# Two attention blocks: the seventh product of the output projection by quarter products

## The chip, the core and the metric

The kernel runs on one core of one Trainium2 chip. Its engines work side by side and wait for one another by semaphores: TensorE (PE in the profile, with its weight loads as PEld), VectorE (DVE), ScalarE (ACT), GpSimd (POOL) and the queue that issues transfers (SPq). Matrix products land in PSUM[...]; operands and results lie in SBUF. The metric is the time of the whole program on the device, in microseconds, median of several runs. Before the change it is 3261.11 us (three runs, 3260.39 to 3261.24).

## What is computed

Two layers of the same kind run one after the other on eight images of 512 channels and 32 x 32 points (N = 1024 tokens), all in float32:

```python
def layer(x, gn_scale, gn_bias, qkv_w, qkv_b, proj_w, proj_b):   # cut to one layer
    xn = group_norm(x) * gn_scale + gn_bias                      # 8 groups, or 32 in the second layer
    q, k, v = split(einsum('oc,bcn->bon', qkv_w, xn) + qkv_b)    # 8 heads of 64
    attn = softmax(einsum('bhdi,bhdj->bhij', q, k) / 8)
    out = einsum('bhij,bhdj->bhdi', attn, v)
    return einsum('oc,bcn->bon', proj_w, out) + proj_b + x       # the output projection
```

The change touches the last line only: the output projection, a product of a 512 x 512 matrix and a 512 x 1024 matrix.

## The kernel before

The kernel goes through 16 units, one for each layer and image. A unit makes q, k and v of its image, then the output projection of the unit before, then its own attention. So there are 15 such projections; that of the last unit is made by another routine with plain products.

Each of q, k, v and the projection is a product of matrices cut into 2 x 2 blocks, made with seven block products instead of eight (the scheme of Strassen and Winograd). A block product is, as it stands, four matmuls of 128 x 128 by 512 columns:

```python
    def block_product(bank, a, b, tokens, start, stop, between=None):
        for i in range(4 if tokens else 2):
            if i == 1 and between is not None:
                between()
            if tokens:
                dst = bank[:, i // 2, (i % 2) * FD2 : (i % 2 + 1) * FD2]
            else:
                dst = bank[:, i, :]
            for c in range(2):
                at, moving = (b, a) if tokens else (a, b)

                nc.tensor.matmul(
                    dst, at[:, c, ts(i, P)], moving[:, c, :],
                    start=start and c == 0 and not (tokens and i % 2),
                    stop=stop and c == 1, skip_group_check=True,
                )
```

Some of the seven are cut into 2 x 2 once more and made by seven quarter products, each one matmul of 256 columns. `INNER` says which:

```python
    INNER = {"q": (2, 5, 4, 3), "k": (1, 2, 7, 5, 4, 3), "o": (2, 3, 4)}
```

The quarter products of one block product go through `inner_products`:

```python
        def inner_products(bank, k, first=False):

            if k not in inner:
                products(bank, k, first, k != 5)
                return None
            a, b, one, two, order, room = inner[k]
            one, two, rest = one[:, 0, :FD2], two[:, 0, :FD2], room(f"m{k}_{name}")
            dst = {
                1: one, 6: one, 7: one, 5: two,
                2: bank[:, 0, :FD2], 3: bank[:, 0, FD2:], 4: bank[:, 1, :FD2],
            }
            to = {
                1: rest[:, 0, :FD2], 6: rest[:, 0, FD2:], 7: rest[:, 1, :FD2], 5: rest[:, 1, FD2:]
            }

            def step(j):
                nc.tensor.matmul(
                    dst[j], a[j], b[j], start=j in (1, 5) or first and j in (2, 4),
                    stop=j not in (1, 6), skip_group_check=True,
                )
                if j in to:
                    taken.append(nc.scalar.copy(to[j], dst[j]))

            for j in order if k != 1 else order[:-1]:
                step(j)
            return (rest, partial(step, order[-1])) if k == 1 else rest

        def fold(rest):
            add = nc.gpsimd.tensor_add
            add(rest[:, 0, FD2:], rest[:, 0, FD2:], rest[:, 1, FD2:])
            add(rest[:, 1, FD2:], rest[:, 1, :FD2], rest[:, 1, FD2:])
```

Quarters 2, 3 and 4 add straight into the bank of the block product. Quarters 1, 6 and 7 go one after the other into the same 256 columns of another bank (`one`), and 5 into a third (`two`). After each of those four ScalarE copies ("takes") what stands there into a room in SBUF, because the partial sums are wanted one by one: 1, 1+6, 1+6+7 and 5. `fold` has GpSimd add the four parts up, and `rests` has it add them to the result. The orders in use are

```python
    ORDER, ORDER_5, ORDER_1 = (1, 2, 3, 6, 5, 4, 7), (1, 5, 2, 6, 3, 4, 7), (2, 3, 1, 4, 5, 6, 7)
```

The first product of k, which uses `ORDER_1`, holds its last quarter back until two matmuls of the next product have gone (`order[:-1]` and `between`). The seven block products follow in this order (those branches that the projection doesn't take are cut):

```python
        bx, by, bz = apair[0], sbank[0], apair[1]
        ...
            products(bx, 1, True, False, between)
            ...
            p1 = work(accpool, "acc", "p1")
            nc.scalar.copy(p1, bx)
            done(sums)
            products(by, 6, True, False)
        u2 = work(*u2_in, "u2")
        summed(0, u2, by, p1)
        done(sums)
        rest = inner_products(bx, 2, fresh)
        c11(bx, p1 if fresh else None, rest)
        add_rest(0, 0, rest)
        done(sums)
        seventh = inner_products(by, 7)
        u3 = work(*u3_in, "u3")
        summed(1, u3, by, p1)
        if seventh is not None:
            fold(seventh)
        done(sums)
        twice = inner_products(bz, 5, True)
        others(1, 1, bz, u3, twice)
        add_rest(1, 1, twice, u3)
        if seventh is not None:
            rests(1, 1, seventh)
        done(sums)
        rest = inner_products(by, 4)
        others(1, 0, by, p1)
        add_rest(1, 0, rest)
        if seventh is not None:
            rests(1, 0, seventh)
        done(sums)
        rest = inner_products(bz, 3)
        others(0, 1, bz, u2, twice)
        add_rest(0, 1, rest, u2 if twice is not None else None)
        if twice is not None:
            rests(0, 1, twice)
        done(sums)
        return taken[-1:]
```

In the projection itself, `c11` and `others` add on VectorE a bank to what is there already; `plus` adds residual and bias; `rests` adds the parts on GpSimd and stores:

```python
        def done(sums):

            nonlocal g
            g += 1
            for i in range(2):
                if g == 2:
                    u2 = sums[1][:, i, :]
                    plus(u2, i, w.res[i][:, FD:], u2)
                elif g == 4:
                    u3 = sums[2][:, i, :]
                    plus(u3, 2 + i, w.res[2 + i][:, FD:], u3)
                elif g == 5:
                    p1 = sums[0][:, i, :]
                    plus(p1, 2 + i, w.res[2 + i][:, :FD], p1)
            after(g)

        results = {}

        def store(o, h):
            nc.sync.dma_start(dst[o * P : (o + 1) * P, ts(h, FD)], results[o, h])

        def c11(bank, *_):
            for i in range(2):
                cols = results[i, 0] = w.res[i][:, :FD]
                plus(cols, i, bank[:, i, :], cols)

        def others(r, h, bank, more, _=None):
            for i in range(2):
                o = 2 * r + i
                results[o, h] = more[:, i, :]
                w.evac[h] = nc.vector.tensor_add(more[:, i, :], bank[:, i, :], more[:, i, :])
                if (r, h) == (1, 1):
                    store(o, h)

        def rests(r, h, rest, _):
            for i in range(2):
                o = 2 * r + i
                cols = results[o, h]
                nc.gpsimd.tensor_add(cols, cols, rest[:, i, :])
                store(o, h)

        w.evac = [None, None]
        x, z, s1 = apair[0], apair[1], sbank[1]
        tmp = room_of(tmppool, "tmp")
        plan = {
            2: (s1, z, ORDER, tmp), 4: (x, s1, ORDER, tmp), 3: (s1, x, ORDER, room_of(accpool, "acc"))
        }
        inner = {k: (*w.inner_o[k], *plan[k]) for k in w.inner_o}
        w.taken = blocks(
            f"o_{w.u}", w.left, w.right_o, False, c11, others, done, (rbpool, "rb"), plain_sum, inner, rests
        )
```

The right factors of the quarters are differences that VectorE makes while v is being projected (numbers such as 20 and 21 in `parts` count the block products done so far: q has 1 to 7, then k 8 to 14, v 15 to 21). The left factors (`lefts`, three per block product) come from memory, where they were put once per layer:

```python
        parts = {
            3: [lambda: reciprocals(CC - 1)], 10: [lambda: divide(CC - 1)], 14: [bias_last],
            17: mixing[:2], 21: [mixing[3], mixing[2]],
        }

        w.inner_o = {}
        l, _ = units[u]
        src = inner_left[l]["o"].rearrange("p k s o -> p (k s) o")
        lefts = []

        def load_left():
            n = 2 * FD // P
            t = trpool.tile([P, n, P], F32, tag="tr", name=f"lo_{u}")
            lefts.extend(t[:, i, :] for i in range(n))
            if u == B:

                w.making = mix_inner_left(l, {"o": left_o})
            else:
                nc.sync.dma_start(t, src[:, :n, :])

        def make_left(i):
            w.making[i](lefts[3 * i : 3 * i + 3], later=behind_loads)

        def mix_o(k):
            tag = {2: "x2", 3: "x1", 4: "x4"}[k]
            room = tpool.tile([P, 4, FD2], F32, tag=tag, name=f"ro{k}_{u}")
            if k == INNER["o"][-1]:
                w.inner_o[k] = mix_inner_in(w.right_o[k], room, nc.vector)
                lefts.append(room[:, 3, :P])
                if u == B:
                    make_left(2)
                else:
                    nc.sync.dma_start(lefts[-1], src[:, len(lefts) - 1, :])
            else:
                w.inner_o[k], subs = mix_inner(w.right_o[k], room, nc.vector)
                for part in subs:
                    part()

        def finish():
            for i, k in enumerate(INNER["o"]):
                w.inner_o[k] = (inner_lefts(k, w.left[k], lefts[3 * i : 3 * i + 3]), w.inner_o[k])

        parts[15] = [load_left]
        if u == B:
            parts[20] = [partial(make_left, 0), partial(make_left, 1)]
        parts[18] = [partial(mix_o, 2)]
        parts[21] += [partial(mix_o, 4), partial(mix_o, 3)]
        w.finish = finish
        return parts
```

Of the kernel before, what the change touches and what calls it, by code (L numbers as in the profile page):

```python
# [11 lines left out]
F32 = mybir.dt.float32  # L12
# [20 lines left out]
def fast_path(ctx, tc, x, qkv_wT, proj_wT, vecs, groups, out, flag):  # L33
# [26 lines left out]

    INNER = {"q": (2, 5, 4, 3), "k": (1, 2, 7, 5, 4, 3), "o": (2, 3, 4)}
    assert D == H and C == FD
# [635 lines left out]
    def project(w, after):  # L698
# [29 lines left out]
        def store(o, h):  # L728
            nc.sync.dma_start(dst[o * P : (o + 1) * P, ts(h, FD)], results[o, h])
# [6 lines left out]
        def others(r, h, bank, more, _=None):  # L736
            for i in range(2):
                o = 2 * r + i
                results[o, h] = more[:, i, :]
                w.evac[h] = nc.vector.tensor_add(more[:, i, :], bank[:, i, :], more[:, i, :])  # L740
                if (r, h) == (1, 1):
                    store(o, h)

        def rests(r, h, rest, _):
            for i in range(2):
                o = 2 * r + i
                cols = results[o, h]
                nc.gpsimd.tensor_add(cols, cols, rest[:, i, :])
                store(o, h)

# [3 lines left out]
        plan = {  # L754
            2: (s1, z, ORDER, tmp), 4: (x, s1, ORDER, tmp), 3: (s1, x, ORDER, room_of(accpool, "acc"))
        }
# [31 lines left out]
    def attention(w, at_step, at_end):  # L788
# [188 lines left out]
        def bias_last():  # L977
# [6 lines left out]
            3: [lambda: reciprocals(CC - 1)], 10: [lambda: divide(CC - 1)], 14: [bias_last],  # L984
            17: mixing[:2], 21: [mixing[3], mixing[2]],
        }
# [19 lines left out]
        def mix_o(k):  # L1006
            tag = {2: "x2", 3: "x1", 4: "x4"}[k]
            room = tpool.tile([P, 4, FD2], F32, tag=tag, name=f"ro{k}_{u}")
            if k == INNER["o"][-1]:
                w.inner_o[k] = mix_inner_in(w.right_o[k], room, nc.vector)  # L1010
                lefts.append(room[:, 3, :P])
                if u == B:
                    make_left(2)
                else:
                    nc.sync.dma_start(lefts[-1], src[:, len(lefts) - 1, :])
            else:
# [7 lines left out]

        parts[15] = [load_left]
        if u == B:
            parts[20] = [partial(make_left, 0), partial(make_left, 1)]
        parts[18] = [partial(mix_o, 2)]
        parts[21] += [partial(mix_o, 4), partial(mix_o, 3)]
        w.finish = finish  # L1030
# [453 lines left out]
```

## Time and profile before

| | |
|---|---|
| time, median of 3 runs | 3261.11 us |
| span of the profiled run | 3260.1 us |
| granted TensorE clock | 1.00 |
| matmuls of quarter products, mean of one record | 379 ns (256 columns) |
| matmuls of whole block products of the projection | 592 ns (512 columns) |
| copies of quarter parts by ScalarE, projection | 180, 372 ns each |
| additions of parts by GpSimd, projection: folds of 256 columns | 90, 735 to 756 ns each on the mean |
| the same: additions of 512 columns to the result | 90, 1268 to 1673 ns each on the mean |

How to read the lines shown later: a line of the timeline gives the start in us from the beginning of the span, the length in us, the engine, the line of the kernel, the operation, what is written and read, and in brackets how long the engine stood idle before and what released it. Neighbouring instructions of one kind are merged, with their number after an x. One float32 matmul of the program leaves two records. Matmuls overlap in the pipeline, so the length of one record is more than the distance to the next. `s` and `a` are banks of PSUM, `m_o` the room for the parts of the projection, `u_o` and `p_o` its sums, `ro` and `lo` right and left factors of quarters. A wait line gives who waited for whom, the total in us, how many times, and the longest.

### The profile page before, as it was taken

Reading aid. Unit: us, or ns where it says so; the run is one execution under the profiler, and the core shown is the slowest. Engines: PE = TensorE matmul, PEld = TensorE weight load, DVE = VectorE, ACT = ScalarE, POOL = GpSimd, SP = SyncE. Lnnn points to the kernel's source line nnn. Section 1 sums busy time; section 2 is a strip of 40 time slices with the busy share of each in tenths; the row PEclk is TensorE's granted clock in tenths of the full one; section 3 lists DMA queues with packets and bytes.
Section 4 is the critical chain, followed back from the end, with each engine's and each line's share of the span. In section 5 each row is a group of like instructions: output and inputs, shape, how many; then the busy total and the mean of one; then the engine's idle time right before and its main releaser. Section 6 shows DMA issues by size and latency. Waiting matters only on the chain.

```text
span 3260.1 us, 56861 instructions
## 1 busy us (share of the span) xinstructions
PE 3247.2 (100%) x22206; PEld 1858.1 (57%) x22206; DVE 2713.7 (83%) x3460; ACT 1650.7 (51%) x2296; POOL 1238.9 (38%) x1235
## 2 busy tenths in 40 slices
PE   9999999999999999999999999999999999999999
PEld 5456474654746547465474655747556474564743
DVE  5887978889788897889978889797897978979777
ACT  1653726536274463744637446374563735637354
POOL 2054071531706317065470632607226071350710
PEclk9999999999999999999999999999999999999999
DMA  3112120121201212023120121201212012120221
GB/s 102 43 52 79 44 78 28 49 79 46 79 28 45 79 46 87 20 71 107 58 89 29 45 80 52 85 15 45 86 46 85 15 49 82 46 85 15 70 74 48
DMA packets 86465, 192.53 MB, mean 59 GB/s; under 512 B 22960, under 2 KB 34992, under 8 KB 84272
## 3 DMA queue, kind: packets, MB, share of 16 engines
q1 hardware_dynamic: 86192, 188.82, 17.0%
q8 instruction: 180, 2.95, 0.4%
q14 instruction: 93, 0.76, 0.1%
HBM read 148.00 MB, written 39.19 MB: 57 GB/s over the span
## 4 chain that ended last, share of the span: by engine, by line
PE 97%; DVE 1%; issue 1%; ACT 0%; DMA 0%; SPq 0%; DVEq 0%; ACTq 0%
PE a L851 26%; PE s L823 25%; PE s L419 14%; PE a L419 12%; PE a L458 10%; PE s L458 9%; PE a L823 1%; DVE acc L870 1%; PE s L769 0%; PE a L769 0%; PE s L364 0%; DVE tr L883 0%; DMA xn<-x_dram 0%; DVE acc L868 0%; ACT p L831 0%
## 5 line engine op out<-in xcount | busy, mean ns | idle before, releaser
L831 ACT ACTIVATE p<-s 128x1024 f32<-128x1024 f32 x976 | 997.0, 1023 | 560.4 <-PE s L823 526.3
L851 PE MATMUL a<-p,v 64*64 64x512 f32 x8192 | 1098.2, 589 | 1.7 <-ACT p L831 1.5
L823 PE MATMUL s<-q,k 64*64 64x512 f32 x7808 | 1056.4, 590 | 0.0
L870 DVE TENSOR_TENSOR acc<-acc,p 128x1024 f32<-128x1024 f32 x768 | 964.0, 1255 | 71.1 <-ACT p L831 18.1
L851 PEld LDWEIGHTS a<-p,v 64*64 64x64 f32 x8192 | 381.0, 131 | 500.5 <-ACT p L831 352.8
L823 PEld LDWEIGHTS s<-q,k 64*64 64x64 f32 x7808 | 380.1, 133 | 435.3 <-issue 425.6
L1080 POOL TENSOR_TENSOR r<-xn 128x256 f32<-128x256 f32 x30 | 51.2, 1707 | 1126.3 <-DVE acc L870 1049.0
L653 POOL TENSOR_TENSOR k<-k,m_k 128x512 f32<-128x512 f32 x180 | 259.7, 1464 | 0.0
L868 DVE TENSOR_TENSOR acc<-p,p 128x1024 f32<-128x1024 f32 x128 | 157.6, 1231 | 23.0 <-ACT p L831 13.9
L883 DVE STREAM_TRANSPOSE tr<-acc 128x1024 f32<-128x1024 f32 x128 | 157.9, 1233 | 0.0
L315 POOL TENSOR_TENSOR y<-var,half 128x4 f32<-128x4 f32 (+1 forms) x17 | 33.1, 1949 | 327.2 <-DVE var L313 327.2
L653 POOL TENSOR_TENSOR q<-q,m_q 128x512 f32<-128x512 f32 x120 | 157.1, 1325 | 0.0
L893 DVE TENSOR_REDUCE red<-tr 128x32 f32<-128x1024 f32 x128 | 153.9, 1202 | 0.5
L541 DVE TENSOR_TENSOR u_v<-s,p_v 128x1024 f32<-128x1024 f32 x32 | 39.2, 1224 | 124.6 <-PE s L419 122.3
L877 DVE TENSOR_TENSOR ao<-a,tmp 128x512 f32<-128x512 f32 x128 | 87.9, 687 | 65.9 <-ACT tmp L876 65.9
L504 ACT COPY p_o<-a 128x1024 f32<-128x1024 f32 x15 | 15.2, 1012 | 244.2 <-PE a L419 244.2
L471 POOL TENSOR_TENSOR m_o<-m_o 128x256 f32<-128x256 f32 x45 | 34.0, 756 | 253.9 <-ACT m_o L463 253.9
L463 ACT COPY m_q<-s 128x256 f32<-128x256 f32 x150 | 55.8, 372 | 145.8 <-PE s L458 143.1
L419 PE MATMUL s<-x_t,s2w 128*128 128x512 f32 x256 | 117.5, 592 | 0.0
L419 PE MATMUL a<-w,xn 128*128 128x256 f32 x496 | 112.1, 379 | 0.0
L463 ACT COPY m_k<-s 128x256 f32<-128x256 f32 x165 | 61.4, 372 | 93.9 <-PE s L458 90.3
L337 ACT ACTIVATE xn<-xn,shift,scale 128x512 f32<-128x512 f32 x124 | 99.5, 804 | 12.4 <-DVE shift L333 12.2
(283 smaller groups left out, 5150.5 us busy)
## 6 DMA issues: line engine op xcount, KB each, us to landing
rb<-drec SPq DMA_DIRECT2D x128, 256.0 KB, 3.8
xn<-mid SPq DMA_DIRECT2D x36, 512.0 KB, 7.6
il<-ilk SPq DMA_DIRECT2D x15, 1152.0 KB, 6.6
xn<-x_dram SPq DMA_DIRECT2D x32, 512.0 KB, 7.2
x<-x_dram SPq DMA_DIRECT2D x32, 512.0 KB, 5.3
x<-mid SPq DMA_DIRECT2D x28, 512.0 KB, 4.8
il<-ilq SPq DMA_DIRECT2D x15, 768.0 KB, 4.2
mid<-u_o SPq DMA_DIRECT2D x32, 256.0 KB, 2.1
```

Of the source, the lines that this page charges most:

```text
L337: nc.scalar.activation(cols, cols, AF.Identity, bias=st["shift"][:, c - lo : c - lo + 1], scale=st["scale"][:, c - lo : c - lo + 1],)
L419: nc.tensor.matmul(dst, at[:, c, ts(i, P)], moving[:, c, :], start=start and c == 0 and not (tokens and i % 2), stop=stop and c == 1, skip ...
L458: nc.tensor.matmul(dst[j], a[j], b[j], start=j in (1, 5) or first and j in (2, 4), stop=j not in (1, 6), skip_group_check=True,)
L463: taken.append(nc.scalar.copy(to[j], dst[j]))
L653: w.last[sel].append(add(cols, cols, rest[:, i, :]))
L823: nc.tensor.matmul(bank[e * H : (e + 1) * H, j, :], w.k[pr][j * H : (j + 1) * H, t * P + e * H : t * P + (e + 1) * H], w.q[pr][j * H : (j ...
L831: exp = nc.scalar.activation(p, bank, AF.Exp, scale=SCALE)
L851: nc.tensor.matmul(banks[r][j * H : (j + 1) * H, :], w.v[rows, t, lo : lo + D], p[rows, j, :], start=(t == 0), stop=(t == NT - 1),)
L868: nc.vector.tensor_add(acc, state["first"], p)
L870: nc.vector.tensor_add(acc, acc, p)
L883: nc.vector.transpose(tr, state["acc"].pop(c))
L893: nc.vector.tensor_reduce(red[:, :, qh, :], state["tr"].rearrange("p j (f i) -> p j f i", i=BL), AX.X, ALU.add)
```

## The change

The seventh block product of the projection, so far four matmuls of 512 columns, is made by seven quarter products of 256 columns too: seven eighths of the columns. Its result is wanted in two blocks of the output, (1,1) and (1,0), so GpSimd adds its parts to both. The block (1,1), which was stored as soon as VectorE had added it, now waits for that addition; the block (1,0) gets the parts of the fourth product and then those of the seventh, and is stored behind the second addition (`to_come` keeps count). The order of quarters is `ORDER_1`. Rooms are found among buffers that are free by then: the parts of the seventh and third products lie in the buffers of two right factors used up by then ("o2", "o1"), the new right factors in an accumulator's buffer ("acc"). Four more left factors' slots are filled, and VectorE makes the right factors of the seventh product one step earlier than those of the fourth and third.

The whole diff:

```diff
--- before.py
+++ after.py
@@ -58,7 +58,7 @@
     BL = 32
     SCALE = 1.0 / math.sqrt(D)
 
-    INNER = {"q": (2, 5, 4, 3), "k": (1, 2, 7, 5, 4, 3), "o": (2, 3, 4)}
+    INNER = {"q": (2, 5, 4, 3), "k": (1, 2, 7, 5, 4, 3), "o": (2, 3, 7, 4)}
     assert D == H and C == FD
 
     def pool(name, bufs, **kw):
@@ -738,21 +738,26 @@
                 o = 2 * r + i
                 results[o, h] = more[:, i, :]
                 w.evac[h] = nc.vector.tensor_add(more[:, i, :], bank[:, i, :], more[:, i, :])
-                if (r, h) == (1, 1):
-                    store(o, h)
-
-        def rests(r, h, rest, _):
+
+
+        to_come = [(1, 0)]
+
+        def rests(r, h, rest, _=None):
             for i in range(2):
                 o = 2 * r + i
                 cols = results[o, h]
                 nc.gpsimd.tensor_add(cols, cols, rest[:, i, :])
-                store(o, h)
+                if (r, h) not in to_come:
+                    store(o, h)
+            if (r, h) in to_come:
+                to_come.remove((r, h))
 
         w.evac = [None, None]
         x, z, s1 = apair[0], apair[1], sbank[1]
         tmp = room_of(tmppool, "tmp")
         plan = {
-            2: (s1, z, ORDER, tmp), 4: (x, s1, ORDER, tmp), 3: (s1, x, ORDER, room_of(accpool, "acc"))
+            2: (s1, z, ORDER, tmp), 7: (s1, z, ORDER_1, room_of(tpool, "o2")),
+            4: (x, s1, ORDER, tmp), 3: (s1, x, ORDER, room_of(tpool, "o1")),
         }
         inner = {k: (*w.inner_o[k], *plan[k]) for k in w.inner_o}
         w.taken = blocks(
@@ -982,7 +987,7 @@
 
         parts = {
             3: [lambda: reciprocals(CC - 1)], 10: [lambda: divide(CC - 1)], 14: [bias_last],
-            17: mixing[:2], 21: [mixing[3], mixing[2]],
+            17: mixing[:2], 20: [mixing[3]], 21: [mixing[2]],
         }
 
         w.inner_o = {}
@@ -1004,15 +1009,16 @@
             w.making[i](lefts[3 * i : 3 * i + 3], later=behind_loads)
 
         def mix_o(k):
-            tag = {2: "x2", 3: "x1", 4: "x4"}[k]
-            room = tpool.tile([P, 4, FD2], F32, tag=tag, name=f"ro{k}_{u}")
-            if k == INNER["o"][-1]:
+            pool, tag = {2: (tpool, "x2"), 7: (accpool, "acc"), 3: (tpool, "x1"), 4: (tpool, "x4")}[k]
+            room = pool.tile([P, 4, FD2], F32, tag=tag, name=f"ro{k}_{u}")
+            if k in (7, 4):
                 w.inner_o[k] = mix_inner_in(w.right_o[k], room, nc.vector)
-                lefts.append(room[:, 3, :P])
-                if u == B:
-                    make_left(2)
-                else:
-                    nc.sync.dma_start(lefts[-1], src[:, len(lefts) - 1, :])
+                n = len(lefts)
+                lefts.extend(room[:, 3, i * P : (i + 1) * P] for i in range(2))
+                if u != B:
+                    nc.sync.dma_start(
+                        room[:, 3, :].rearrange("p (s o) -> p s o", s=2), src[:, n : n + 2, :]
+                    )
             else:
                 w.inner_o[k], subs = mix_inner(w.right_o[k], room, nc.vector)
                 for part in subs:
@@ -1023,10 +1029,12 @@
                 w.inner_o[k] = (inner_lefts(k, w.left[k], lefts[3 * i : 3 * i + 3]), w.inner_o[k])
 
         parts[15] = [load_left]
+        parts[18] = [partial(mix_o, 2)]
+        parts[20].append(partial(mix_o, 7))
+        parts[21] += [partial(mix_o, 4), partial(mix_o, 3)]
         if u == B:
-            parts[20] = [partial(make_left, 0), partial(make_left, 1)]
-        parts[18] = [partial(mix_o, 2)]
-        parts[21] += [partial(mix_o, 4), partial(mix_o, 3)]
+            parts[20] += [partial(make_left, i) for i in range(3)]
+            parts[21].append(partial(make_left, 3))
         w.finish = finish
         return parts
```

## The prediction

> **What bounds the kernel now.** I read the busy times first, then the waits by engine, then the instructions in order of time around one output projection.
>
> ```profile
> PE 3247.2 (100%) x22206; PEld 1858.1 (57%) x22206; DVE 2713.7 (83%) x3460; ACT 1650.7 (51%) x2296; POOL 1238.9 (38%) x1235
> ```
>
> TensorE (PE) is busy for 3247.2 of 3260.1 us. A busy PE need not be a PE at its peak, so the waits of PE must say whether anything holds it:
>
> ```profile
> PE s L364 <- DMA xn<-x_dram: 4.3, 1, 4.3
> PE a L851 <- ACT p L831: 1.5, 1, 1.5
> PE s L295 <- DVE mv L287: 0.4, 1, 0.4
> PE s L419 <- DVE xn L179: 0.3, 1, 0.3
> ```
>
> These are all of them: 6.5 us, nearly all at the start. So the time is the sum of what PE is given, and a change is worth what it takes from or adds to PE's own sequence. Everything on the other engines matters only if PE comes to wait for it. The next view is PE's timeline in one projection (of image 1, while image 2 is prepared). The second column is the length of a merged run; the pace is the distance between starts:
>
> ```profile
> 479.83 3.60 PE L419 MATMUL s<-ao,wproj_wproj 128*128 128x512 f32 x8
> 483.27 3.60 PE L419 MATMUL a<-o_t,s1w 128*128 128x512 f32 x8
> 486.70 0.59 PE L458 MATMUL a<-o_t,wproj_wproj 128*128 128x256 f32 x2
> ```
>
> The first line is the seventh product, today four plain matmuls of 512 columns (two records each): it takes PE 483.27 - 479.83 = 3.44 us, and the fifth behind it 3.43. The second product, already done by quarter products, shows what the new form costs and where its copies lie (all engines; lines left out are marked):
>
> ```profile
> 476.81 0.59 PE L458 MATMUL s<-ao,wproj_wproj 128*128 128x256 f32 x2
> ...
> 477.44 0.37 ACT L463 COPY m_o<-s 128x256 f32<-128x256 f32 x1 [2.81 <-PE s L458]
> ...
> 478.11 0.59 PE L458 MATMUL s<-ro,lo 128*128 128x256 f32 x2
> ...
> 478.54 0.59 PE L458 MATMUL a<-ro,lo 128*128 128x256 f32 x2
> ...
> 478.74 0.37 ACT L463 COPY m_o<-s 128x256 f32<-128x256 f32 x1 [0.92 <-PE s L458]
> ...
> 479.40 0.59 PE L458 MATMUL s<-ro,wproj_wproj 128*128 128x256 f32 x2
> ...
> 479.83 1.02 PE L419 MATMUL s<-ao,wproj_wproj 128*128 128x512 f32 x2
> ```
>
> Seven quarter products go from 476.81 to 479.83: 3.02 us, 0.431 each, with no gap. They run in the order 1, 2, 3, 6, 5, 4, 7. Quarters 1, 6 and 7 add up in the same columns of one bank (s), and ScalarE must copy each partial sum out before the next is added. The copy of quarter 1 starts 0.63 us after that quarter starts (477.44 - 476.81), that of quarter 6 likewise (478.74 - 478.11), and each lasts 0.37. So such a sum is free again 1.00 us after its quarter started. Quarter 7 comes three places behind 6, 1.29 us after it; the copy has ended 0.29 us before, and nothing waits.
>
> **What the Trainium skill says.** "PSUM — Partial Sum Buffer", section "PSUM bank collisions raise a hardware error": a matmul that writes a bank and another engine that reads it must be kept apart by a semaphore, by bank and not by address. The timeline agrees as far as it goes: every copy lies between the matmuls on its bank. "TensorE: Matmul & The Clock Gate", section "Step-by-step: what each phase is for": weights are loaded ahead, while the matmul before runs. The trace agrees, with loads of quarters some 0.2 us ahead of their matmul; and it shows what is lost when a wait forbids that, in the next fence. "Perfetto Trace Analysis", section "Tensor Engine Instruction (MATMUL, LD_WEIGHTS)": the end of a matmul record is an estimate, so I take only starts. "SBUF — State Buffer", section "Who interferes with whom": a VectorE addition of two SBUF operands and a GpSimd operation block one another. The trace agrees: a subtraction of 128x256 takes 0.42 us alone (475.60) and 0.94 beside GpSimd's additions (463.97).
>
> **Part 1: fewer columns on PE.** In each of the 15 projections that are made by seven products (the sixteenth is made plainly), the seventh goes from 3.44 to 3.02 us: -0.42 us. 15 x 0.42 = -6.2 us. If nothing waits, the time is 3261.1 - 6.2 = 3254.9.
>
> **Part 2: the new order makes one wait.** The seventh product uses the order 2, 3, 1, 4, 5, 6, 7. Starting with 2 and 3 is well chosen: quarter 1 goes into the bank from which the second product's last quarter is still being copied, and the two places give that copy its 1.00 us (start of quarter 1 less start of that quarter: 3 x 0.431 = 1.29). But 6 and 7 now stand side by side, and in the list of the changed kernel's instructions with their waits both carry a wait for ScalarE. Quarter 7 would start 0.43 us after 6; the copy of 6 ends only 1.00 after it. What a restart costs besides is seen at the one place of the kernel before where a quarter just fails to get its copy in time:
>
> ```profile
> 232.94 0.36 ACT L463 COPY m_k<-a 128x256 f32<-128x256 f32 x1
> ...
> 233.35 0.30 PEld L458 LDWEIGHTS a<-k,il 128*128 128x128 f32 x2 [0.24 <-ACT m_k L463]
> 233.35 0.70 PE L458 MATMUL a<-k,il 128*128 128x256 f32 x2
> ...
> 233.88 0.38 PE L458 MATMUL s<-k,il 128*128 128x256 f32 x1
> ```
>
> The copy ends at 233.30, weights and matmul both start 0.05 later, and the pair lasts 0.70 instead of 0.59 (the next quarter comes after 0.53 instead of 0.43): 0.10 us for weights that could not be loaded ahead. So quarter 7 costs 1.00 + 0.05 + 0.10 - 0.43 = 0.72 us of standing still. ScalarE is free for the copy: the copies of 1 and 5 end before it is due (quarter 5's runs from 0.20 to 0.57 us after quarter 6 starts). Per projection: -0.42 + 0.72 = +0.30 us; 15 of them, +4.5 us.
>
> **Part 3: work beside PE.** Per projection four more copies on ScalarE (4 x 0.372 = 1.5 us; it was busy 5.1 of 22.9 us there). On GpSimd two folds at 0.73 and four additions at about 1.27: 6.5 us, 98 us in all, 1239 to some 1337. On VectorE four subtractions of 0.42, 1.7 us, and one of 1.22 moved forward, between the last two sums of v. VectorE idled 2.23 us there (its sum at 470.14), so 2.9 us push the last sum of v back by 0.7 us. That bank is wanted again by the second product's quarter 5, at 478.5, and v itself in the attention: nothing on PE waits. GpSimd's last addition ended at 498.57, six us into the attention; now the (1,1) block, free at about 488.6, and 2 x 1.27 more for (1,0) carry it to some 502. The first attention steps need none of it: their accumulator takes the buffer of the new right factors, which TensorE has left by then, and the second accumulator comes only at 508. VectorE's additions there lengthen from 1.23 to about 1.49 beside GpSimd, still under TensorE's 1.72 per step. The stores of the (1,1) block leave some 3 us later, far from the end. Cost on the path: 0, with up to 0.5 us for making the extra left factors in two images.
>
> **The sum.** 3261.1 - 6.2 + 15 x 0.72 = 3261.1 - 6.2 + 10.8 = 3265.7 us.
>
> **Rivals.** (a) The wait is hidden or much shorter, and only part 1 is left: 3254.9. For it: the same order is in use for the first product of k. Against: there the last quarter is held back behind two matmuls of the next product, and here it isn't. (b) The extra GpSimd work reaches the path: additions that end later block VectorE, exponentials wait for buffers, and PE for them; a loss of 0.5 us per image would make it 3273. For it: VectorE is busy 90% of the projection (20.8 of 22.9 us). Against: in the first 14 us of attention it is busy 11.7, the sums it makes for PE stand ahead of GpSimd's, and no wait of PE for it is on the page. (c) The wait is there without the weight penalty, 0.62 us or less, if the load is let through ahead: 3264 or a little under.
>
> **Range and chances.** Everything turns on one wait of 0.55 to 0.9 us in 15 places against a sure 6.2 us: 3263 to 3268.5, and I widen it downward for part of (a), upward for some of (b): 3259.5 to 3269.5. Two per cent would be 65 us, which neither side of the sum can reach: within 2% 0.985, faster 0.005, slower 0.01.
>
> **What would show each step.** In the timeline: the seventh product's first six quarters 0.43 us apart, then 1.05 (weight load and matmul together) to quarter 7 and 0.53 behind it; the product 3.74 us from first quarter to the fifth product. In the waits, 15 new waits of quarter products for copies of m_o, or a gap of PE's weight loads put down to ScalarE. GpSimd some 98 us busier, PE busier only by record overlap. Wrong would be: no gap ahead of quarter 7 (then rival a), or a first attention step that starts late, or exponentials that wait for VectorE in the first chunk (rival b).

## The result, and the profile after

The changed kernel takes 3274.09 us (median of 4 runs, 3273.87 to 3275.62), the kernel before 3261.18 beside it. The ratio is 1.0041 (95% interval 1.0023 to 1.0058): 12.9 us slower, where the prediction had 4.6 us (3265.7 against 3261.1) and a range that ended at 3269.5.

The busy times of the changed kernel, and then its waits of PE, in the same form as those of before (engine, bank and line, releaser; us in total, times, longest):

```profile
PE 3249.1 (99%) x22296; PEld 1945.1 (59%) x22296; DVE 2807.1 (86%) x3520; ACT 1675.4 (51%) x2356; POOL 1420.6 (43%) x1333
```

```profile
PE s L458 <- ACT m_o L463: 6.9, 15, 0.5
PE s L364 <- DMA xn<-x_dram: 4.3, 1, 4.3
PE a L828 <- DVE u_o L740: 2.3, 13, 0.3
PE a L856 <- ACT p L836: 2.0, 2, 1.8
PE a L295 <- DVE e L308: 1.0, 1, 1.0
PE s L828 <- POOL m_o L472: 0.5, 1, 0.5
...
PE s L458 <- DVE u_o L541: 0.4, 1, 0.4
```

Two waits are new in nearly every unit. One is the predicted one, quarter products for ScalarE's copies, 15 times. The other was not: scores of the attention (L828, into bank `a`) for VectorE's last sum of the projection. A wait line counts only the time in which PE stands idle; what a late restart costs in pace is seen in the starts. GpSimd is 182 us busier (prediction: 98), VectorE 93.

The first wait, in the projection of the unit that starts its attention at 493 us (units counted from 0, this is unit 2): the last two quarters of the seventh product, ScalarE's copy between them, and the fifth product behind.

```profile
482.40 0.59 PE L458 MATMUL s<-ro,lo 128*128 128x256 f32 x2
...
483.04 0.37 ACT L463 COPY m_o<-s 128x256 f32<-128x256 f32 x1
...
483.46 0.30 PEld L458 LDWEIGHTS s<-ao,wproj_wproj 128*128 128x128 f32 x2 [0.86 <-ACT m_o L463]
483.46 0.70 PE L458 MATMUL s<-ao,wproj_wproj 128*128 128x256 f32 x2 [0.46 <-ACT m_o L463]
...
484.00 3.60 PE L419 MATMUL a<-o_t,s1w 128*128 128x512 f32 x8
```

Quarter 6 starts at 482.40, its copy ends at 483.41, quarter 7 starts at 483.46, 1.06 us after 6 (predicted 1.05), and the fifth product 0.54 later (predicted 0.53). The product begins at 480.25, so it takes 3.75 us (predicted 3.74).

The second wait, at the end of the same projection. First four lines of the kernel before, then those of the changed one (L823 and L828 are the scores: the first go into `s`, the third into `a`):

```profile
488.16 1.41 DVE L706 SCALAR_TENSOR_TENSOR p_o<-x,vec,p_o 128x512 f32<-128x512 f32 x2
...
492.51 1.29 DVE L740 TENSOR_TENSOR u_o<-a,u_o 128x512 f32<-128x512 f32 x2 [0.54 <-PE a L458]
...
492.84 1.95 PE L823 MATMUL s<-q,k 64*64 64x512 f32 x16
...
494.60 1.04 PE L823 MATMUL a<-q,k 64*64 64x512 f32 x8
```

```profile
488.46 2.94 POOL L749 TENSOR_TENSOR u_o<-u_o,m_o 128x512 f32<-128x512 f32 x2 [2.49 <-DVE u_o L740]
...
488.89 3.06 DVE L706 SCALAR_TENSOR_TENSOR p_o<-x,vec,p_o 128x512 f32<-128x512 f32 x2
...
493.57 1.95 PE L828 MATMUL s<-q,k 64*64 64x512 f32 x16
...
494.27 1.26 DVE L740 TENSOR_TENSOR u_o<-a,u_o 128x512 f32<-128x512 f32 x2
...
495.65 0.24 PEld L828 LDWEIGHTS a<-q,k 64*64 64x64 f32 x8 [1.01 <-DVE u_o L740]
495.68 1.09 PE L828 MATMUL a<-q,k 64*64 64x512 f32 x8 [0.16 <-DVE u_o L740]
```

GpSimd's two additions to (1,1) (L749) are new at this place. They start 0.43 us ahead of VectorE's two residual additions to the next block (L706), which take 3.06 us instead of 1.41. VectorE's last sum, of block (0,1), now starts at 494.27, 0.70 us after the first scores (493.57); before it started 0.33 us ahead of them (492.51 against 492.84). So it is 1.03 us later against PE. Before, it had ended 0.80 us before the third scores wrote its bank; now they must wait and start 2.11 us after the first, 0.34 us late. The first chunk of the attention becomes 0.37 us longer. In unit 15, which prepares no next image, the pair takes 3.06 us too; but no statistics stand ahead of the last sum there, it starts 0.33 us ahead of the first scores, and the third are on time (1.77).

A unit's attention goes in 64 steps, each with scores, exponentials and a product with v, and eight steps are a chunk. The first chunk is measured from the first scores to the start of the ninth product with v, each later one from there over eight products more. Cut into stretches by the starts of PE's matmuls, the trace gives this (us; the twelve plain units are 1 to 6, 8 and 10 to 14):

| | before | after | sum of the differences |
|---|---|---|---|
| start of projection to first scores, plain units and 15 | 22.89 | 23.21 | 13 x 0.32 = 4.2 |
| first to third scores, plain units | 1.77 | 2.11 | (in the next line) |
| first chunk of attention, plain units | 15.50 | 15.87 | 12 x 0.37 = 4.4 |
| unit 7: projection; first, second chunk; the rest | 22.89; 15.50, 13.91; 82.07 | 23.47; 15.61, 15.40; 82.87 | 3.0 |
| unit 9: projection; first chunk | 22.89; 15.50 | 24.46; 16.03 | 2.1 |

The sum is 13.7, the spans differ by 3273.8 - 3260.1 = 13.7 us (the medians by 12.9; the run with the profile was the longest of the four). Unit 7 is the one in which the second layer's weights are prepared, unit 9 the one in which GpSimd makes the left factors of that layer's projection (twelve, where it made nine before).

### The profile page after: what moved, and what is told of

It is laid out like the page before. It is cut to its first block, busy times and chain, and to the rows that moved or that the text cites. A ratio compares the mean times of both kernels' runs of the same rounds, so it can differ in the third digit from the quotient of the medians.

```text
span 3273.8 us, 57367 instructions
## 1 busy us (share of the span) xinstructions
PE 3249.1 (99%) x22296; PEld 1945.1 (59%) x22296; DVE 2807.1 (86%) x3520; ACT 1675.4 (51%) x2356; POOL 1420.6 (43%) x1333
## 5 line engine op out<-in xcount | busy, mean ns | idle before, releaser
L856 PE MATMUL a<-p,v 64*64 64x512 f32 x8192 | 1121.2, 589 | 2.2 <-ACT p L836 2.0
L828 PE MATMUL s<-q,k 64*64 64x512 f32 x7808 | 1078.3, 590 | 0.5 <-POOL m_o L472 0.5
L875 DVE TENSOR_TENSOR acc<-acc,p 128x1024 f32<-128x1024 f32 x768 | 1003.2, 1306 | 68.7 <-ACT p L836 12.9
L856 PEld LDWEIGHTS a<-p,v 64*64 64x64 f32 x8192 | 408.5, 131 | 473.6 <-ACT p L836 331.3
L828 PEld LDWEIGHTS s<-q,k 64*64 64x64 f32 x7808 | 423.9, 133 | 392.9 <-issue 380.3
L471 POOL TENSOR_TENSOR m_o<-m_o 128x256 f32<-128x256 f32 x60 | 65.9, 1098 | 169.0 <-ACT m_o L463 168.9
L749 POOL TENSOR_TENSOR u_o<-u_o,m_o 128x512 f32<-128x512 f32 x60 | 109.8, 1853 | 34.1 <-DVE u_o L740 34.1
L463 ACT COPY m_o<-s 128x256 f32<-128x256 f32 x150 | 55.9, 373 | 113.2 <-PE s L458 110.5
```

What stands on the lines that cost most here:

```text
L828: nc.tensor.matmul(bank[e * H : (e + 1) * H, j, :], w.k[pr][j * H : (j + 1) * H, t * P + e * H : t * P + (e + 1) * H], w.q[pr][j * H : (j ...
L856: nc.tensor.matmul(banks[r][j * H : (j + 1) * H, :], w.v[rows, t, lo : lo + D], p[rows, j, :], start=(t == 0), stop=(t == NT - 1),)
L875: nc.vector.tensor_add(acc, acc, p)
```

## The experiments

All start from the changed kernel unless another is named. "Projection", "third scores" and "chunk" mean the stretches of the table. A summary first; each ratio is to runs of the kernel before on the same chip.

| kernel | time, us | ratio, 95% interval | projection | third scores | second chunk |
|---|---|---|---|---|---|
| changed | 3274.09 | 1.0041 [1.0023, 1.0058] | 23.21 | 2.11 | 13.91 |
| hold7 | 3268.31 | 1.0022 [1.0013, 1.0030] | 22.78 | 2.11 | 13.91 |
| no_add11 | 3270.00 | 1.0026 [1.0016, 1.0036] | 23.21 | 1.77 | 13.91 |
| no_add10 | 3272.65 | 1.0035 [1.0022, 1.0047] | 23.21 | 2.11 | 13.91 |
| early_p1 | 3270.98 | 1.0031 [1.0019, 1.0042] | 23.21 | 1.77 | 13.91 |
| late_add11 | 3280.58 | 1.0060 [1.0043, 1.0077] | 23.21 | 1.77 | 14.69 |
| order7 | 3264.71 | 1.0012 [1.0005, 1.0018] | 22.48 | 2.12 | 13.91 |
| order_early | 3269.28 | 1.0025 [1.0015, 1.0035] | 22.48 | 1.77 | 14.50 |
| order_late | 3271.99 | 1.0034 [1.0022, 1.0047] | 22.48 | 1.77 | 14.69 |
| early_shift | 3266.90 | 1.0017 [1.0010, 1.0023] | 22.48 | 1.77 | 14.10 |
| early_shift_make | 3267.26 | 1.0017 [1.0010, 1.0024] | 22.48 | 1.77 | 14.11 |
| stats_shift | 3263.22 | 1.0005 [0.9997, 1.0013] | 22.48 | 1.77 | 13.91 |
| stats_by | 3261.11 | 0.9998 [0.9990, 1.0007] | 22.48 | 1.77 | 13.91 |
| stats_one | 3259.20 | 0.9995 [0.9987, 1.0004] | 22.48 | 1.77 | 13.91 |

**hold7: the wait inside the seventh product.** Its last quarter is held back behind two matmuls of the fifth product, as the first product of k does it.

```diff
-            for j in order if k != 1 else order[:-1]:
+            held = k == 1 or k == 7 and name[0] == "o"
+            for j in order[:-1] if held else order:
...
-        twice = inner_products(bz, 5, True)
+        if last is None:
+            twice = inner_products(bz, 5, True)
+        else:
+            twice = products(bz, 5, True, False, last)
+            fold(seventh)
```

> The seventh product's last quarter is held back behind two matmuls of the fifth product, so that its copy wait falls away. Two-term theory (0.72 us of standing still ahead of quarter 7 in 15 projections, and apart from it 0.34 us ahead of the third scores in 14 units, which follows VectorE's sums and these follow the fifth product): 3274.1 - 15 x 0.72 = 3263.3 us, seventh to fifth product in 3.02 us plus the held quarter's 0.43, third scores still 0.34 us late. Rival, VectorE's and GpSimd's own work sets when the third scores may start: the gap there grows from 0.34 to about 1.06 us and the time stays at 3273 to 3274.

3268.31 us. The wait of 0.72 has gone, but only 0.43 of it is saved in each projection, since the fifth product now meets another one. In the timeline of hold7, quarters 5 and 6, the copy of 5, and the fifth product:

```profile
480.25 0.59 PE L458 MATMUL a<-ro,lo 128*128 128x256 f32 x2
480.69 0.59 PE L458 MATMUL s<-ro,lo 128*128 128x256 f32 x2
480.89 0.37 ACT L463 COPY m_o<-a 128x256 f32<-128x256 f32 x1 [0.49 <-PE a L458]
...
481.31 0.30 PEld L419 LDWEIGHTS a<-o_t,s1w 128*128 128x128 f32 x2 [0.43 <-ACT m_o L463]
481.31 1.98 PE L419 MATMUL a<-o_t,s1w 128*128 128x512 f32 x4
```

The fifth product writes the bank into which quarter 5 went (480.25), and with 7 taken out it comes two places behind it, where a copy needs 1.00 us: 481.31 - 480.25 = 1.06 again. So the rule of the prediction (a partial sum is free 1.00 us after its quarter starts, three places of 0.43 are enough and two aren't) holds at a second place. The third scores are as late as ever: the two waits don't depend on one another.

**no_add11 and no_add10: which of GpSimd's additions.** Each leaves out the seventh product's parts from one of the two blocks, so that block of the output lacks them; it is stored behind the addition that is then its last.

```diff
-        if seventh is not None:
+        if seventh is not None and name[0] != "o":
             rests(1, 1, seventh)       # no_add11; in no_add10 the same ahead of rests(1, 0, seventh)
```

> GpSimd leaves out the additions of the seventh product's parts to block (1,1), which is stored behind VectorE's sum as before; the output lacks these parts. Theory that just these additions block VectorE's two residual additions to p1 (3.06 us instead of 1.41) and with them the sum for which the third scores wait: the pair takes 1.4 us, the gap of 0.34 us ahead of the third scores is gone in all units: 3274.1 - 14 x 0.34 = 3269, or up to 3 us less if units 7 and 9 recover too. Rival, that it is GpSimd's later end in the attention: additions end some 2.5 us sooner, but the pair and the gap stay as they are: 3273 to 3274. Quarter 7's stall of 0.72 us stays in both.

> GpSimd leaves out the additions of the seventh product's parts to block (1,0) instead, stored behind the fourth product's parts; the output lacks them. Same amount of work taken off GpSimd as in the run without the additions to (1,1), but later in time. Theory that the additions to (1,1) do it: gap ahead of the third scores stays 0.34 us, 3272 to 3274. Rival, the later end of GpSimd's work: gap gone, 3269.

3270.0 and 3272.65 us. Without the additions to (1,1) the third scores start at 1.77 in the plain units and the first chunk is 15.50; without those to (1,0), as many additions less, they stay at 2.11. It is not the amount of GpSimd's work but the two additions that meet VectorE's. The additions to (1,0) have a cost of their own in unit 7 alone: its second chunk falls from 15.40 to 14.27. Those to (1,1) cost in unit 9 too: without them its projection falls from 24.46 to 23.84 and its first chunk from 16.03 to 15.50.

**early_p1: the same work, VectorE's part moved.** The two residual additions to `p1` go right behind those to `u3`, which GpSimd's additions to (1,1) don't meet. Nothing is left out.

```diff
-                elif g == 5:
+            for i in range(2):
+                if g == 4:
                     p1 = sums[0][:, i, :]
```

> Nothing is left out; VectorE makes the two residual additions to p1 right behind those to u3, while TensorE still makes the fifth product and GpSimd has not begun its additions to (1,1). Theory that the additions of two operands in SBUF are blocked there: the pair takes 1.4 to 2 us in its new place, VectorE's sums of products 4 and 3 come some 1.6 us sooner, the gap ahead of the third scores is gone: 3269. Rival, VectorE has too much work there whatever its order (four subtractions more per projection): the gap stays or moves to the fourth product, 3273 to 3275.

3270.98 us. The timeline of early_p1, unit 2:

```profile
484.94 1.40 DVE L706 SCALAR_TENSOR_TENSOR p_o<-x,vec,p_o 128x512 f32<-128x512 f32 x2
...
487.62 2.50 POOL L750 TENSOR_TENSOR u_o<-u_o,m_o 128x512 f32<-128x512 f32 x2 [3.15 <-DVE u_o L741]
...
491.76 1.29 DVE L741 TENSOR_TENSOR u_o<-a,u_o 128x512 f32<-128x512 f32 x2 [0.54 <-PE a L458]
```

Both pairs have the length they have alone, VectorE's last sum starts 0.32 us ahead of the first scores (492.08) again, and the third scores are not late in any unit. With no_add11 this shows the cause of the wait at the third scores: two operations met in time. Of the 4.4 us that the plain units had lost by it, 3.1 appear in the median: VectorE now comes late in unit 7 (projection 24.44, second chunk 15.56) and unit 9 (24.20, 14.86).

**late_add11: the same work, GpSimd's part moved.**

```diff
-        if seventh is not None:
-            rests(1, 1, seventh)
...
         if seventh is not None:
             rests(1, 0, seventh)
+            rests(1, 1, seventh)
```

> As the changed kernel, but GpSimd's two additions to the (1,1) block come behind those to (1,0): the same work, at another time, not beside VectorE's two residual additions. Theory (the third scores wait because these additions meet): the pair of residual additions takes 1.4 us again, third scores 1.77 us after the first, first chunk 15.50; projection 23.21; 3269 us, or up to 3 us more if GpSimd's later end (some 510 in the unit that starts at 493) delays sums in the second chunk. Rival (it is the amount of GpSimd's work in the projection, not its meeting with these two): third scores stay late, 3273 to 3274.

3280.58 us, worse than any other, although the third scores are not late. The theory was right on its point and its forecast wrong: the waits show a new one, the matmul that sums the next image's statistics over a group (L295), 14 times.

```profile
PE a L295 <- DVE e L308: 6.3, 14, 0.6
```

GpSimd's additions to (1,1) now lie in the attention as well, and VectorE's additions there, `acc<-acc,p`, read two SBUF operands too: in unit 2 the first two of them take 4.33 us instead of 3.78. VectorE comes late with `e`, and PE stands ahead of that matmul. The second chunk is 14.69: 0.78 more in each of the twelve plain units.

**order7: the wait taken away wholly.** As hold7, and the order of the seventh product is 2, 3, 1, 5, 4, 6, 7.

```diff
-            2: (s1, z, ORDER, tmp), 7: (s1, z, ORDER_1, room_of(tpool, "o2")),
+            2: (s1, z, ORDER, tmp), 7: (s1, z, (2, 3, 1, 5, 4, 6, 7), room_of(tpool, "o2")),
```

> The seventh product's quarters in the order 2, 3, 1, 5, 4, 6, 7, with 7 held back behind two matmuls of the fifth product. Quarter 6 then stands three places behind 1, and the fifth product starts three places behind quarter 5, so every copy has 1.29 us and needs 1.00. Theory (the standing still is only the copy's 1.00 us against the places given): no wait is left inside or behind the seventh product, projection 22.48 us from its start to the first scores (22.89 before, 23.21 after, 22.78 with 7 alone held back); third scores still 2.11 us after the first; 3274.1 - 15 x 0.72 = 3263.3 us. Rival (two quarters on one bank or the held-back quarter cost PE something else): a gap of 0.1 to 0.3 us per projection stays, 3265 to 3268.

3264.71 us. In the timeline of order7, from quarter 1 to the fifth product:

```profile
478.52 0.59 PE L458 MATMUL s<-ao,wproj_wproj 128*128 128x256 f32 x2
478.96 0.59 PE L458 MATMUL a<-ro,lo 128*128 128x256 f32 x2
...
479.39 0.59 PE L458 MATMUL s<-ro,wproj_wproj 128*128 128x256 f32 x2
...
479.82 0.59 PE L458 MATMUL s<-ro,lo 128*128 128x256 f32 x2
480.25 1.88 PE L419 MATMUL a<-o_t,s1w 128*128 128x512 f32 x4
```

Every start is 0.43 us from the last; the projection takes 22.48 us, just 0.41 less than before. So part 1's saving is there in full once no copy is waited for. The time is 1.4 us above the 3263.3 expected. The trace shows 1.1 of it: units 7 and 9 take 23.16 and 24.42, so of the 0.73 that the new order saves on PE only 0.31 and 0.03 came out; there VectorE sets the pace (see stats_one).

**order_early and order_late: both waits taken away.** order7 with the edit of early_p1, and order7 with that of late_add11.

> The same order with 7 held back, and VectorE's two residual additions to p1 ahead of GpSimd's additions to the (1,1) block. Theory (the steady loss is the sum of the two waits, 0.72 per projection and 0.37 per attention, and both are taken away): projection 22.48 and third scores 1.77 us after the first in the units without preparation for the second layer; 3274.1 - 10.8 - 3.1 (what the early additions alone gave) = 3260.2 us, as fast as the kernel before, with what is left of 6.2 us of saving lost in the two units around the change of layers. Rival (the waits are exchanged for others, for PE reaches the attention sooner than VectorE): third scores late again by 0.1 to 0.4 us, 3262 to 3266.

> The order of quarters of order7 with GpSimd's (1,1) additions behind those to (1,0). Theory: projection 22.48, third scores at 1.77: 3274.1 - 10.8 - 5 = 3258 us, with some of it lost again around the change of layers; up to 3261 if GpSimd's later end delays the second chunk. Rival: as for the two changes alone, 3262 or more.

3269.28 and 3271.99 us. Both theories fell. The waits were exchanged for others, as the rival to order_early had it, but at another place than it named and for more time. Projection (22.48) and third scores (1.77) are as wanted, and yet order_early is slower than order7. The waits and the timeline of order_early:

```profile
PE a L295 <- DVE e L308: 5.9, 14, 0.6
```

```profile
514.61 0.15 DVE L302 COPY mean<-a 128x4 f32<-128x4 f32 x1
...
515.19 0.16 DVE L308 TENSOR_TENSOR e<-d,mv 128x4 f32<-128x4 f32 x1
...
515.50 0.22 PE L295 MATMUL a<-e,gmat 64*64 64x4 f32 x2 [0.42 <-DVE e L308]
```

This is the wait of late_add11, met without its edit. PE arrives in the attention 1.1 us earlier than in the changed kernel, VectorE doesn't: beside GpSimd, which adds until 505.5 (until 498.6 before), its first seven additions of `acc` take 1.80 us on the mean in most plain units (1.38 before, 1.73 in the changed kernel). The second chunk is 0.59 longer. So the waits taken away had given VectorE time that it now takes elsewhere.

**early_shift, early_shift_make and stats_shift: does VectorE lack time, or is it only late?** early_shift is order_early with the statistics' matmuls and arithmetic one or two steps later in the attention; stats_shift takes, in place of the early residual additions, two statistics of VectorE from ahead of its last sum to behind it; early_shift_make moves GpSimd's making of left factors for unit 9.

```diff
-            elif c == 1 + late and t == 3:
+            elif c == 1 + late and t == 4:
                 means(abank[2 * pair], *free)
-            elif c == 1 + late and t == 5:
+            elif c == 1 + late and t == 6:
                 variances(abank[2 * pair], *free)
-            elif c == 2 + late and t == 0:
+            elif c == 2 + late and t == 2:
                 scales()
-            stats_after = {3: (0, 1, 2), 4: (3,), 6: (4, 5), 7: (6, 7)}
+            stats_after = {3: (0, 1, 2), 4: (3,), 7: (4, 5, 6, 7)}      # stats_shift only
```

> As order_early (order of quarters mended, VectorE's residual additions to p1 early), and in the attention the two small matmuls of the next image's group statistics and the scale arithmetic one or two steps later (means at step 4, variances at 6 of the second chunk, scales at step 2 of the third). Theory: in order_early VectorE has only come late by its additions beside GpSimd, and the matmul of the variances waited 0.6 us for it because it stands at a fixed place in PE's order; one step later (1.72 us) nothing waits. Second chunk 13.91 again in the 12 undisturbed units, projection 22.48: 3269.3 - 12 x 0.59 = 3262, and about 1 us less around the change of layers: 3261 us. Rival (VectorE is short of time, not late, and the wait moves on): second or third chunk still 0.3 us or more too long, 3266 or more.

> As early_shift, but instead of the early residual additions two of VectorE's statistics of the next image stand behind its last sum of the projection instead of ahead of it, so that the sum comes 1.27 us earlier. Theory: the third scores need that sum 0.35 us earlier than they got it; they start 1.77 us after the first although the residual additions still take some 3 us beside GpSimd; projection 22.48, second chunk 13.91: 3264.7 - 14 x 0.37 = 3259.5 us, 3258 to 3261. Rival (the time lost beside GpSimd must come out somewhere on PE): second chunk longer by 0.3 us, 3263 or more.

> As early_shift, and GpSimd makes the left factors of the second layer's first projection at other places, one by one from the third product of v on, instead of three of them just ahead of VectorE's last subtractions. Theory (the subtractions of VectorE lengthen beside GpSimd's making, 0.42 to some 0.6 us): the projection of unit 9 loses its 1.7 us over 22.48, or most of it; 1.5 us below early_shift. Rival (the loss there is GpSimd's sum of work before the projection): unit 9 unchanged.

3266.90, 3263.22 and 3267.26 us. In stats_shift the plain units have neither wait: 22.48, 1.77, 15.50, 13.91. VectorE's pair still takes 3.06 us beside GpSimd; the sum behind it comes in time because two statistics, 1.27 us, now stand behind it and not ahead of it. So VectorE was late, not short of time. In early_shift 0.2 us of the statistics' wait is left per unit: between theory and rival. Both were spoilt by the edit itself in unit 0, whose own places for this work are one chunk later: there the third and fourth chunk went from 14.19 + 14.16 to 13.91 + 18.58 in stats_shift, 4.1 us. early_shift_make changed nothing (unit 9: 24.32 against 24.34). The timeline says why: in both, GpSimd is busy with k until the moment when it makes the first left factor, so an earlier place in its program isn't an earlier time. That theory falls, as far as the remedy goes; the making still lies beside VectorE's subtractions, which take 0.56 to 0.68 us there instead of 0.42.

**stats_by and stats_one: what is left.** stats_shift without the edit in unit 0; stats_by moves the work in unit 7 by two steps, stats_one by one as elsewhere.

```diff
+            by = 0 if late else 2 if u == B - 1 else 1      # stats_one: 0 if late else 1
-            elif c == 1 + late and t == 4:
+            elif c == 1 + late and t == 3 + by:
```

> As stats_shift, but the later place of the next image's statistics not in the first unit, whose own places are others (there the move alone cost 4.1 us: third and fourth chunk 13.91 + 18.58 instead of 14.19 + 14.16), and two steps later instead of one in the unit that prepares the second layer, where the variances still waited 1.37 us. Theory: 3263.2 - 4.1 - 1.3 = 3257.8 us; the projection 22.48, third scores 1.77, second chunk 13.91 in every unit but those two around the change of layers, and what is still lost of the 6.2 us saved stands in these two. Rival: the wait in the unit before the second layer is GpSimd's or VectorE's lack of time, moves to the third chunk, and the time stays at 3259 or more.

> As stats_by, but one step later instead of two in the unit that prepares the second layer. Theory (that unit is short of VectorE and GpSimd time, so its wait of some 1.3 us in the second chunk stays, but the 4.0 us that stats_by lost in the third chunk there came from the move by two steps and goes): third chunk of unit 7 13.73, second some 15.3; 3261.1 - 4.0 = 3257.1 us, 3256.5 to 3258.5, below the kernel before by some 4 us: 6.2 saved, about 5 lost in the two units around the change of layers, less what other waits of before are not met. Rival (the loss is the same wherever it is met): 3260 to 3261.5.

3261.11 and 3259.20 us. In stats_by the rival won: unit 7's second chunk stays long (15.52) and its third becomes 17.73 instead of 13.73. The timeline of stats_by there:

```profile
1537.67 0.81 ACT L337 ACTIVATE xn<-xn,shift,scale 128x512 f32<-128x512 f32 x1 [2.54 <-DVE shift L333]
1538.39 1.92 ACT L843 ACTIVATE p<-s 128x1024 f32<-128x1024 f32 x2
...
1539.54 1.98 PE L863 MATMUL a<-p,v 64*64 64x512 f32 x8 [2.05 <-ACT p L843]
```

ScalarE stood 2.54 us for the late `shift`, the exponentials stood behind it in its queue, and PE behind them. In stats_one the third chunk is 13.73 as expected, but the median is only 1.9 us lower, not 4.0. The two traces differ by 3.1 (spans 3261.0 and 3257.9), for 1.3 us come back at the end of unit 7, where the kernel before has a wait for exponentials too (last chunk 12.07 in stats_by, 13.37 in stats_one, 13.35 before). The rest is between runs: they ran on two chips, and beside their own runs of the kernel before they stand 0.1 and 1.4 us below. stats_one takes 3259.20 us where the kernel before takes 3260.63, ratio 0.9995 [0.9987, 1.0004]: not shown to be faster. The waits of stats_one:

```profile
PE s L364 <- DMA xn<-x_dram: 4.4, 1, 4.4
PE a L863 <- ACT p L843: 1.5, 1, 1.5
PE s L835 <- POOL m_o L473: 1.3, 1, 1.3
PE a L295 <- DVE e L308: 1.2, 1, 1.2
PE s L458 <- DVE u_o L548: 0.5, 1, 0.5
```

The first two are there before too; the third and fifth are unit 9's, the fourth unit 7's. The third is that of the first scores, and the profile puts it down to a fold of GpSimd's. But the kernel has the first scores wait for VectorE's sum of (1,0), not for a fold, and in unit 9 they start 0.26 us after that sum ends here and in order_late alike: here the fold had ended 0.07 us before, there GpSimd's last operation 2.0 us before. So VectorE is late here too.

In all, 13 projections gain 0.37 to 0.41 us, 5.3 together, and two units give 3.3 back: unit 7's projection and second chunk are 0.26 and 1.39 us longer than before, unit 9's projection 1.68. That leaves 2.0; the spans differ by 2.2.

## Why the prediction was wrong

- **Part 1 was right.** Without any wait the projection is 0.41 us shorter (order7), predicted 0.42.
- **Part 2 was right, term for term:** 1.06 for 1.05 us from quarter 6 to 7, 3.75 for 3.74 for the product, 15 waits, the projection 0.32 longer for 0.30. Its 15 x 0.32 = 4.8 us are the 4.6 of the sum (which has 6.2 for 15 x 0.42; that is 6.3, and 6.2 with the 0.41 measured).
- **Part 3 is the step that failed:** "Cost on the path: 0, with up to 0.5 us for making the extra left factors in two images". It cost about 9 us: 12 x 0.37 = 4.4 in the plain units, and about 4.5 in units 7 and 9 above the 0.32 that each shares with the rest. In the plain units the runs showed what it is: VectorE's residual additions meet GpSimd's additions to (1,1), take 3.06 us instead of 1.41, and VectorE's last sum frees its bank too late for the third scores. Three things led there. First, "the sums it makes for PE stand ahead of GpSimd's": true of the first of them, while VectorE's last sum for PE, of (0,1), comes 5.8 us after the additions to (1,1) begin, and it had only 0.80 us to spare. Second, "On GpSimd ... 98 us in all": it was 182, for a record's length holds the time in which the operation is kept out; the folds take 1.07 us on the mean instead of 0.75, and in unit 2 GpSimd adds until 507.06, 13.5 us into the attention, instead of "some 502", 9 us into it. Third, VectorE's side of the same meeting was counted for `acc` alone ("about 1.49"; the first seven take 1.73 on the mean); the residual additions, which also read two SBUF operands, were not looked at.
- **The rivals.** (b) was the right direction, and its size near (0.5 us per image written, 0.37 found), with a way that was not quite the one named: not late exponentials, but a bank that VectorE frees late. That its total of 3273 came near is luck: half of what part 3 cost lies in two units, of which (b) says nothing. It was put aside because VectorE's busy time left room. A share of busy time says nothing about the one instruction that PE waits for. (a) and (c) were wrong: the wait is there, with its 0.10 for weights.
- **A line misread.** Of the 6.5 us of waits "nearly all at the start", the 1.5 for exponentials stand at the end of unit 7, in its last chunk (13.35 us; 11.67 in a plain unit). That unit was tight before the change, and it is one of the two that lost most.
- **The range** was widened upward to 3269.5 "for some of (b)"; all of (b) needed 3273, as the text itself reckoned.
- **Not settled:** about half of the 4.5 us in units 7 and 9. no_add10 takes 1.1 off unit 7's second chunk (GpSimd's additions to (1,0)), no_add11 takes 1.1 off unit 9 (those to (1,1)). Which of their other pieces of work makes VectorE late in these two is not shown.

## What to carry to other kernels

Before giving a helper engine more work, list the instructions of its neighbour that read two SBUF operands at the same time, and for each find the next thing that the bottleneck engine waits for and how much time to spare it had. A wait taken away from the bottleneck engine makes it arrive earlier at the next place where it meets a late helper: look at the slack there before counting the gain. A partial sum that must be copied out needs a fixed time (here 1.00 us) measured in places of the sequence (here three), and an order of instructions can be chosen by counting places.

## What the runs showed of the hardware

The Trainium skill ("SBUF — State Buffer", section "Who interferes with whom") calls the port pair that VectorE's second SBUF operand shares with GpSimd an exclusive lock, in which the later instruction blocks for as long as the first one lasts. The trace agrees. In unit 2 the two pairs, one instruction a line, take turns:

```profile
488.46 1.27 POOL L749 TENSOR_TENSOR u_o<-u_o,m_o 128x512 f32<-128x512 f32 x1 [2.49 <-DVE u_o L740]
...
488.89 1.38 DVE L706 SCALAR_TENSOR_TENSOR p_o<-x,vec,p_o 128x512 f32<-128x512 f32 x1
...
489.69 1.72 POOL L749 TENSOR_TENSOR u_o<-u_o,m_o 128x512 f32<-128x512 f32 x1
...
490.20 1.75 DVE L706 SCALAR_TENSOR_TENSOR p_o<-x,vec,p_o 128x512 f32<-128x512 f32 x1
```

They end at 489.73, 490.27, 491.41 and 491.95. The first addition of GpSimd keeps its length alone, 1.27; the three others end 0.54, 1.14 and 0.54 us after the one ahead of them, a little less than their lengths alone (0.75 on VectorE, 1.27 on GpSimd): nearly all of their work came when the other was done. In the view of the tile `p_o` (shortest, median and longest of 30, in ns), first the kernel before, then the changed one:

```profile
L706 DVE SCALAR_TENSOR_TENSOR p_o<-x,vec,p_o x30: 743/746/941, 286.6 to 3112.1; 128x512 f32<-128x512 f32 x30
```

```profile
L706 DVE SCALAR_TENSOR_TENSOR p_o<-x,vec,p_o x30: 932/1385/1755, 286.7 to 3126.0; 128x512 f32<-128x512 f32 x30
```

An addition of 0.75 us becomes 1.39 or 1.75 when it meets one of GpSimd's, of 1.27. And the sums that read one operand from PSUM keep their 0.68 us in the same stretch (two take 1.29 at 486.96 before, where GpSimd is idle, and 1.26 at 494.27 after, where it adds): which operand lies where decides.
